# Layer 3's weight products in a four-layer graph kernel: ahead of layer 0, or in pieces inside its aggregation

## The chip, the cores and the metric

The kernel runs on one core of one Trainium2 chip. The metric is the device time of one execution in microseconds (us), less being better. TensorE (PE) does matmuls, VectorE (DVE) and ScalarE (ACT) work on vectors, GpSimd (POOL) on vectors and transfers, and SyncE (SP) sends most transfers (DMAs).

## The reference

Four graph layers work on x (2708 x 512, fp32) with one adjacency matrix adj (2708 x 2708, 0 or 1). Each normalizes x by rows, applies a relu, and adds its result to x. Cut to what matters here:

```python
# layer 0, h = relu(layernorm(x))
x = x + relu(((adj.T @ h) @ weight) * in_degree ** -0.5)
# layer 3, deg = rows' sums of adj
agg = adj @ h / deg
self_f = h @ W_self + b_self
nb_f = agg @ W_nb + b_nb
x = x + relu(concat(self_f, nb_f) @ W_comb + b_comb)
```

Nothing but linear steps lies between `W_self` or `W_nb` and `W_comb`. So the kernel makes the products `W_self @ W_comb[:512]` and `W_nb @ W_comb[512:]` once (each 512 x 512 x 512, fp32) and one row of bias, and layer 3 multiplies with these.

## The kernel before

`fast_layers` cuts the 2708 nodes into 22 chunks of 126 rows (NC = 22, R = 126; the last has 62). D = 512 columns make NF = 4 blocks of 128.

**Ahead of layer 0** (lines 321 to 375). A pool "pre" takes `W_self`, `W_comb`, `W_nb` and the biases. `turn_weight` transposes one weight: four blocks on TensorE into one PSUM bank (L341), and a copy by ACT to `wsT` (L342), four times. `fuse` makes 128 rows of one product in four fp32 matmuls (L347), and DVE copies them to `wf` (L354). When a product is whole, POOL's queue sends it to `fused` in DRAM (L356, 1 MB). DVE sums the rows of `W_comb`, weighted by the biases, into `part` (L367, L369), TensorE adds its partitions (L373), and the row goes to `bias3` (L375). Layer 3 reads `fused` and `bias3` some 800 us later.

**Layer 0** (lines 467 to 668) has six groups of column chunks, of 4, 4, 4, 4, 3 and 3 chunks; in the text they are groups 1 to 6 (g = 0 to 5 in the code). One unit is a group and a row chunk m: 6 x 22 = 132 units. `staged` calls every stage with a lag: at step s, a stage of lag k handles unit s - k. `load0` (lag 0) brings the adjacency tile `ai`, 126 rows by the group's columns, int32, from ten buffers. `count0` (lag 4) makes the matmul weight `ar` of it on ACT (L523), and on DVE a running count (L529), a degree (L537) and a packed pair of rows `two` (L541). `sign0` (lag 5) counts on ACT (L557). `multiply0` (lag 7) sends `two` to DRAM by POOL's queue (L574) and multiplies `ar` with the chunk's features into one PSUM accumulator per column chunk (L403, two matmuls each since a feature is held as a high and a low half). In the first group only, `dense` also runs: load x (lag 0), normalize (lag 1: L216, L218, L220, L221, L230), transpose on TensorE with a relu on ACT (lag 2: L239, L241), and multiply with the layer's weight `w0s` (lag 3: L186, four fp32 matmuls), then the two halves (L292 on ACT, L293 on DVE). At the end of a group the accumulators are scaled and added to x (L611 to L648); `fenced` puts the next group's `count0` and `sign0` behind these instructions on DVE and ACT.

**What orders the work.** The code gives a sequence and priorities. A scheduler simulates the program when it is built, and gives each engine and each queue a fixed order: what is ready goes, the earlier in the code the sooner. Work from far down can so come early. In the run each engine takes its order strictly, and a transfer waits in its queue until its buffer is free, with all behind it. The PSUM pool `ps` has eight banks, shared by accumulators, transposes and products.

**Layer 1's start** (lines 670 to 769) needs the degrees of all chunks: they go to DRAM and back (L685 to L692), and DVE waits for them at L695.

Of the kernel before, what the change touches and what calls it, by code (L numbers as in the profile page):

```python
# [20 lines left out]
P = 128  # L21
# [23 lines left out]
def fast_layers(  # L45
# [278 lines left out]
    with tc.tile_pool(name="pre", bufs=2) as pre:  # L324
        ws = [load_weight(pre, w_self, "ws")]
        wc = load_weight(pre, w_comb, "wc", k=2 * NF)
        ws.append(load_weight(pre, w_nb3, "ws"))
        bc = load_row(pre, b_comb, "bc")
        bcol = pre.tile([P, 2 * NF], F32, name="bcol")
        for i, b in enumerate((b_self, b_nb3)):  # L330
            nc.sync.dma_start(
                bcol[:, i * NF : (i + 1) * NF], b.rearrange("(k p) -> p k", p=P)
            )
        wsT = [pre.tile([P, NF, D], F32, name="wsT") for _ in range(2)]
        wf = [pre.tile([P, NF, D], F32, name="wf") for _ in range(2)]

        def turn_weight(i):
            for f in range(NF):
                pt = ps.tile([P, NF, P], F32, name="wsT_ps", tag="ps")
                for k in range(NF):  # L340
                    nc.tensor.transpose(pt[:, k, :], ws[i][:, f, k * P : (k + 1) * P], ident)  # L341
                nc.scalar.copy(wsT[i][:, :, f * P : (f + 1) * P], pt)  # L342

        def fuse(i, f):
            po = ps.tile([P, D], F32, name="fused_ps", tag="ps")
            for k in range(NF):
                nc.tensor.matmul(  # L347
                    po,
                    wsT[i][:, k, f * P : (f + 1) * P],
                    wc[:, i * NF + k, :],  # L350
                    start=(k == 0),
                    stop=(k == NF - 1),
                )
            nc.vector.tensor_copy(wf[i][:, f, :], po)  # L354
            if f == NF - 1:
                nc.gpsimd.dma_start(fused[i].rearrange("(k p) o -> p k o", p=P), wf[i])  # L356

        turn_weight(0)
        for f in range(NF):
            if f == NF // 2:  # L360
                turn_weight(1)
            fuse(0, f)
        for f in range(NF):
            fuse(1, f)

        part = pre.tile([P, D], F32, name="part", bufs=1)
        nc.vector.tensor_scalar(part, wc[:, 0, :], bcol[:, 0:1], None, op0=ALU.mult)  # L367
        for k in range(1, 2 * NF):
            nc.vector.scalar_tensor_tensor(  # L369
                part, wc[:, k, :], bcol[:, k : k + 1], part, op0=ALU.mult, op1=ALU.add  # L370
            )
        pb = ps.tile([P, D], F32, name="bias3_ps", tag="ps")
        nc.tensor.matmul(pb[:1], ones, part, start=True, stop=True)  # L373
        nc.vector.tensor_tensor(bc[:1], pb[:1], bc[:1], ALU.add)
        nc.gpsimd.dma_start(bias3, bc[:1])  # L375
# [76 lines left out]
    with ExitStack() as ring_ctx:  # L452
# [14 lines left out]
        w0s = load_weight(weights, w0, "w0s", tag="w")  # L467
# [10 lines left out]
        def product0(c, xc, hT, n):  # L478
            po = ps.tile([P, D], F32, name="h0_ps", tag="ps")
            any_product(c, po, hT, w0s, n)  # L480
            h0[c] = halves(ring, po, c)

        with tc.tile_pool(name="l0", bufs=2) as wk:
# [173 lines left out]
            def first_dense(lag, fn):  # L657
                return lag, lambda i: fn(i) if i < NC else None

            staged(  # L660
                len(units),
                (0, load0),
                *[first_dense(lag, fn) for lag, fn in dense(x_in, product0, rows_of=paired)],
                (4, fenced(count0)),
                (5, fenced(sign0)),
                (7, save0),
# [1365 lines left out]
```

## Time and profile before

| What | us |
|---|---|
| Median of 3 runs | 1805.42 |
| Lowest and highest run | 1805.1, 1805.82 |
| Span of the profiled execution, first to last instruction | 1804.1 |
| TensorE busy in it | 1767.0 |
| DVE, ACT, POOL busy | 1308.8, 815.3, 247.3 |
| First matmul; first transpose of layer 0 | 3.37; 38.78 |
| First adjacency tile sent | 47.64 |
| First accumulation matmul of layer 0 | 59.56 |
| Last accumulation matmul of layer 0 starts | 376.92 |

The page has no device time of its own for the profiled execution; its span is 1.3 us below the median. Each digit in the slices of the page is the busy share, in tenths, of a fortieth of the span (45.1 us). A line of a timeline has the start, the duration, the engine, the line of code, the operation, what it writes and reads, and how many instructions were merged; brackets hold the idle time of the engine before it, and what released it. Matmuls are pipelined, so the durations of single ones overlap, and a rate is read from a run of them.

### The profile page before, as it was taken

What the parts mean: (1) busy time and instruction counts of PE and PEld (TensorE: products, weight loads), DVE (VectorE), ACT (ScalarE), POOL (GpSimd) and SP (SyncE); (2) the same over time, 40 slices, a digit from 0 to 9 for tenths busy, and PEclk for the clock granted to TensorE, in tenths of its full rate; (3) what the DMA queues carried; (4) which work ended last, traced back from release to release, by engine and by line L of the source; (5) the groups of instructions that cost most, each with busy time, mean ns of one, the idle gap of its engine ahead of it and who ended that gap; (6) DMA issues with size and microseconds to landing.
All of it is one profiled execution on the core that took longest, in us unless ns stands there. A gap on an engine that the chain in (4) does not pass through costs nothing.

```text
span 1804.1 us, 30724 instructions
## 1 busy us (share of the span) xinstructions
PE 1767.0 (98%) x11880; PEld 1039.3 (58%) x11880; DVE 1308.8 (73%) x1842; ACT 815.3 (45%) x1554; POOL 247.3 (14%) x245
## 2 busy tenths in 40 slices
PE   9899999899999999999999999999999899999998
PEld 4456777654447887744444344344444445588776
DVE  4952998855546665788989999999999777633334
ACT  2643777731210000056887777767774566400000
POOL 0100332311110211157000000000000222100000
PEclk9999999999999999999999999999999999999999
DMA  7632666735552221243320220121122444313221
GB/s 249 191 103 80 205 207 188 216 72 123 122 123 62 62 69 53 66 154 107 102 62 13 57 60 24 47 62 43 28 63 56 137 138 134 116 33 105 70 69 45
DMA packets 165737, 176.62 MB, mean 98 GB/s; under 512 B 94890, under 2 KB 116100, under 8 KB 164700
## 3 DMA queue, kind: packets, MB, share of 16 engines
q1 hardware_dynamic: 143170, 131.47, 26.4%
q10 hardware_dynamic: 18668, 33.28, 5.4%
q0 software_dynamic: 3744, 9.82, 1.6%
q8 instruction: 95, 1.56, 0.4%
q14 instruction: 60, 0.49, 0.1%
HBM read 111.35 MB, written 55.15 MB: 92 GB/s over the span
## 4 chain that ended last, share of the span: by engine, by line
PE 80%; DVE 10%; issue 4%; DMA 4%; ACT 1%; POOL 0%; SPq 0%; DVEq 0%; ACTq 0%; POOLq 0%
PE acc L403 32%; PE av L1110 16%; PE nb_ps L186 7%; PE sums L1110 5%; DVE t L923 5%; PE self_ps L186 4%; PE line_ps L186 4%; PE wh_ps L186 3%; PE h_ps L186 3%; DVE cum L529 2%; PE hT_ps L239 2%; PE fused_ps L347 2%; DMA x<-x 1%; DMA ai<-in_adj 1%; DMA x<-in_x 1%
## 5 line engine op out<-in xcount | busy, mean ns | idle before, releaser
L923 DVE SCALAR_TENSOR_TENSOR t<-rb,ec,vT 126x2708 f32<-126x2708 f32 (+2 forms) x220 | 529.5, 2464 | 13.4 <-PE sums L1110 7.7
L403 PE MATMUL acc<-halves,kt 126*126 126x512 f32 x1848 | 435.7, 395 | 2.3 <-DVE kt L777 2.0
L1110 PE MATMUL av<-t,whs 126*32 126x451 f32 (+3 forms) x4576 | 433.5, 513 | 0.6 <-DVE ln_mv L218 0.6
L403 PEld LDWEIGHTS acc<-halves,kt 126*126 126x126 f32 x1848 | 342.6, 186 | 91.7 <-DVE kt L777 6.8
L1110 PEld LDWEIGHTS av<-t,whs 126*32 126x32 f32 (+1 forms) x4576 | 162.4, 110 | 200.7 <-issue 175.2
L403 PE MATMUL acc<-halves,ar 126*126 126x512 f32 x924 | 232.3, 404 | 3.4 <-ACT ar L523 2.0
L941 ACT ACTIVATE b<-t,eb 126x2708 bf16<-126x2708 f32 (+3 forms) x91 | 217.8, 2393 | 34.6 <-DVE t L923 32.9
L403 PEld LDWEIGHTS acc<-halves,ar 126*126 126x126 f32 x924 | 169.0, 186 | 53.8 <-issue 7.6
L220 ACT ACTIVATE ln_rs<-ln_mv,eps 126x1 f32<-126x1 f32 x88 | 25.6, 293 | 327.5 <-DVE ln_mv L218 323.3
L777 DVE SCALAR_TENSOR_TENSOR kt<-lastr,index,vT 126x504 fp32r<-126x504 int16 (+3 forms) x154 | 110.7, 731 | 78.6 <-PE acc L403 78.2
L1349 DVE CAST kt<-vT 126x504 fp32r<-126x504 uint8 (+3 forms) x154 | 56.1, 366 | 137.0 <-PE acc L403 137.0
L1077 POOL TENSOR_SCALAR z<-y 126x512 f32<-126x512 f32 x22 | 44.0, 2000 | 652.8 <-DVE y L1070 644.1
L1110 PE MATMUL sums<-t,whs 126*32 126x338 f32 (+4 forms) x1464 | 129.6, 447 | 2.7 <-ACT out L1151 2.7
L529 DVE TENSOR_TENSOR_SCAN cum<-ai,deg 126x504 int16<-126x504 int32 (+2 forms) x110 | 128.5, 1181 | 0.7 <-DMA ai<-in_adj 0.7
L911 ACT ACTIVATE whs<-wh,ef 126x64 f32<-126x64 f32 x220 | 76.6, 348 | 101.2 <-PE sums L1110 47.0
L557 ACT ACTIVATE cum<-cum,limit 126x504 int16<-126x504 int16 (+3 forms) x132 | 88.1, 668 | 58.9 <-DVE deg L537 57.9
L216 DVE BATCH_NORM_STATS2 ln_st<-x 126x6 f32<-126x512 f32 x88 | 60.4, 686 | 45.7 <-DMA x<-x 29.7
L1110 PEld LDWEIGHTS sums<-t,whs 126*32 126x32 f32 (+1 forms) x1464 | 52.6, 109 | 65.1 <-issue 35.9
L186 PE MATMUL h_ps<-w0s,hT 128*126 128x512 f32 x168 | 79.0, 614 | 5.5 <-ACT hT L241 4.2
L186 PE MATMUL nb_ps<-wfn,hT 128*126 128x512 f32 x168 | 75.7, 593 | 3.2 <-ACT hT L241 3.2
L186 PE MATMUL nb_ps<-wn,hT 128*126 128x512 f32 x168 | 76.6, 599 | 0.0
L523 ACT ACTIVATE ar<-ai 126x504 fp32r<-126x504 int32 (+2 forms) x132 | 74.9, 567 | 3.0 <-DMA ai<-in_adj 3.0
(202 smaller groups left out, 1885.6 us busy)
## 6 DMA issues: line engine op xcount, KB each, us to landing
x<-x SPq DMA_DIRECT2D x105, 252.0 KB
x<-x ACTq DMA_DIRECT2D x84, 252.0 KB
ai<-in_adj SPq DMA_DIRECT2D x84, 249.0 KB
x<-in_x SPq DMA_DIRECT2D x42, 252.0 KB
rb<-rT SPq DMA_DIRECT2D x7, 1332.8 KB
wh<-whd SPq DMA_DIRECT2D x70, 94.5 KB
packed<-two POOLq DMA_DIRECT2D x44, 124.5 KB, 4.4
whd<-wh SPq DMA_DIRECT2D x21, 252.0 KB
```

The source lines that it names most:

```text
L186: nc.tensor.matmul(po[:n], lhsT[:, f, :n], w[:, f, :], start=(f == 0), stop=(f == NF - 1))
L216: nc.vector.bn_stats(st[:n], xc[:n])
L403: nc.tensor.matmul(acc[:R], weight[:, k * R : (k + 1) * R], parts[:, i, :], start=(m == 0 and i == 0), stop=(m == NC - 1),)
L523: nc.scalar.activation(ar[:, :gw], ai[:, :gw], AF.Square, accum_out=squares[:R, m, g : g + 1])
L529: nc.vector.tensor_tensor_scan(cum[:n, :gw], ai[:n, :gw], ai[:n, :gw], 0.0 if g == 0 else deg[:n, m : m + 1], op0=ALU.add, op1=ALU.max,)
L557: nc.scalar.activation(cum[:n, :gw], cum[:n, :gw], AF.Sign, bias=limit[:n], scale=-1.0, accum_out=signs[:n, m, g : g + 1],)
L777: nc.vector.scalar_tensor_tensor(by_chunk(kt, cs), lastr[:, cs[0] * R : (cs[-1] + 1) * R].rearrange("p (c r) -> p c r", r=R), index[:R, m ...
L911: ins = nc.scalar.activation(t[:q, :O], wh.pop((u, m))[:q], AF.Copy, scale=by)
L923: ins = nc.vector.scalar_tensor_tensor(t[:q, : hi - lo], row[h][:q, lo:hi], ec[:q, m, h : h + 1], vT[g][:q, k, lo:hi], op0=ALU.max, op1=AL ...
L941: nc.scalar.activation(b[:q, : hi - lo], weight[s][:q, : hi - lo], AF.Sigmoid, bias=eb[:q, m, h : h + 1], scale=STEEP,)
L1110: nc.tensor.matmul(p[j * S : (j + 1) * S, : b - a], lhsT, rhs[:, part * size + a : part * size + b], start=(s % NC == 0), stop=(s % NC == ...
L1349: nc.vector.tensor_copy(by_chunk(kt, cs), pattern(m, cs))
```

## The change

The pool "pre" and its block go. A class `Fusion` holds the same work in pieces: `load`, `turn` (four transposes and an ACT copy), `multiply` (one fp32 matmul; the fourth of a row block also copies the block by ACT, not DVE, and sends its 256 KB on POOL's queue), `add` (one step of the bias row on DVE), `close`. Its buffers are single, except for `wf` with two, and lie beside layer 0's in a pool of their own. A table assigns pieces to units, and a last stage of lag 7 runs them after `multiply0` of that unit: product i = 0 in groups 2 and 3 (4 turns and 8 multiplies, then 8 multiplies), product i = 1 in groups 4 and 5 in the same way, from the third step of a group to its eighteenth; the adds in the last four units of groups 1 and 3; the close in group 6. The weights of a product are asked for ten units ahead of its first group. `w0s` is loaded in the first step, after the first x chunk and before the first adjacency tile; x comes ahead of adj in every step of the first group.

```diff
@@ -321,58 +321,65 @@
 
     bias3 = dram.tile([1, D], F32, name="bias3")
     fused = [dram.tile([D, D], F32, name=f"fused{i}") for i in range(2)]
-    with tc.tile_pool(name="pre", bufs=2) as pre:
-        ws = [load_weight(pre, w_self, "ws")]
-        wc = load_weight(pre, w_comb, "wc", k=2 * NF)
-        ws.append(load_weight(pre, w_nb3, "ws"))
-        bc = load_row(pre, b_comb, "bc")
-        bcol = pre.tile([P, 2 * NF], F32, name="bcol")
-        for i, b in enumerate((b_self, b_nb3)):
-            nc.sync.dma_start(
-                bcol[:, i * NF : (i + 1) * NF], b.rearrange("(k p) -> p k", p=P)
+
+    class Fusion:
+        def __init__(self, pool):
+            self.pool = pool
+            self.ws, self.wc, self.wsT, self.po = {}, {}, {}, {}
+
+        def load(self, i):
+            self.ws[i] = load_weight(self.pool, (w_self, w_nb3)[i], "ws")
+            self.wc[i] = load_weight(self.pool, w_comb[i * D : (i + 1) * D, :], "wc")
+            if i == 0:
+                self.bcol = self.pool.tile([P, 2 * NF], F32, name="bcol")
+                for j, bias in enumerate((b_self, b_nb3)):
+                    nc.sync.dma_start(
+                        self.bcol[:, j * NF : (j + 1) * NF], bias.rearrange("(k p) -> p k", p=P)
+                    )
+                self.bc = self.pool.tile([1, D], F32, name="bc")
+                nc.sync.dma_start(self.bc, b_comb.rearrange("(o d) -> o d", o=1))
+
+        def turn(self, i, f):
+            if f == 0:
+                self.wsT[i] = self.pool.tile([P, NF, D], F32, name="wsT")
+            pt = ps.tile([P, NF, P], F32, name="wsT_ps", tag="ps")
+            for k in range(NF):
+                nc.tensor.transpose(pt[:, k, :], self.ws[i][:, f, k * P : (k + 1) * P], ident)
+            nc.scalar.copy(self.wsT[i][:, :, f * P : (f + 1) * P], pt)
+
+        def multiply(self, i, f, k):
+            if k == 0:
+                self.po[i, f] = ps.tile([P, D], F32, name="fused_ps", tag="ps")
+            po = self.po[i, f]
+            nc.tensor.matmul(
+                po,
+                self.wsT[i][:, k, f * P : (f + 1) * P],
+                self.wc[i][:, k, :],
+                start=(k == 0),
+                stop=(k == NF - 1),
             )
-        wsT = [pre.tile([P, NF, D], F32, name="wsT") for _ in range(2)]
-        wf = [pre.tile([P, NF, D], F32, name="wf") for _ in range(2)]
-
-        def turn_weight(i):
-            for f in range(NF):
-                pt = ps.tile([P, NF, P], F32, name="wsT_ps", tag="ps")
-                for k in range(NF):
-                    nc.tensor.transpose(pt[:, k, :], ws[i][:, f, k * P : (k + 1) * P], ident)
-                nc.scalar.copy(wsT[i][:, :, f * P : (f + 1) * P], pt)
-
-        def fuse(i, f):
-            po = ps.tile([P, D], F32, name="fused_ps", tag="ps")
-            for k in range(NF):
-                nc.tensor.matmul(
-                    po,
-                    wsT[i][:, k, f * P : (f + 1) * P],
-                    wc[:, i * NF + k, :],
-                    start=(k == 0),
-                    stop=(k == NF - 1),
-                )
-            nc.vector.tensor_copy(wf[i][:, f, :], po)
-            if f == NF - 1:
-                nc.gpsimd.dma_start(fused[i].rearrange("(k p) o -> p k o", p=P), wf[i])
-
-        turn_weight(0)
-        for f in range(NF):
-            if f == NF // 2:
-                turn_weight(1)
-            fuse(0, f)
-        for f in range(NF):
-            fuse(1, f)
-
-        part = pre.tile([P, D], F32, name="part", bufs=1)
-        nc.vector.tensor_scalar(part, wc[:, 0, :], bcol[:, 0:1], None, op0=ALU.mult)
-        for k in range(1, 2 * NF):
+            if k == NF - 1:
+                wf = self.pool.tile([P, D], F32, name="wf", bufs=2)
+                nc.scalar.copy(wf, self.po.pop((i, f)))
+                nc.gpsimd.dma_start(fused[i][f * P : (f + 1) * P, :], wf)
+
+        def add(self, i, k):
+            col = self.bcol[:, i * NF + k : i * NF + k + 1]
+            if (i, k) == (0, 0):
+                self.part = self.pool.tile([P, D], F32, name="part")
+                nc.vector.tensor_scalar(self.part, self.wc[i][:, k, :], col, None, op0=ALU.mult)
+                return
             nc.vector.scalar_tensor_tensor(
-                part, wc[:, k, :], bcol[:, k : k + 1], part, op0=ALU.mult, op1=ALU.add
+                self.part, self.wc[i][:, k, :], col, self.part, op0=ALU.mult, op1=ALU.add
             )
-        pb = ps.tile([P, D], F32, name="bias3_ps", tag="ps")
-        nc.tensor.matmul(pb[:1], ones, part, start=True, stop=True)
-        nc.vector.tensor_tensor(bc[:1], pb[:1], bc[:1], ALU.add)
-        nc.gpsimd.dma_start(bias3, bc[:1])
+
+        def close(self):
+            pb = ps.tile([P, D], F32, name="bias3_ps", tag="ps")
+            nc.tensor.matmul(pb[:1], ones, self.part, start=True, stop=True)
+            nc.vector.tensor_tensor(self.bc, pb[:1], self.bc, ALU.add)
+            nc.gpsimd.dma_start(bias3, self.bc)
 
 
 
@@ -464,7 +471,7 @@
             ],
         )
 
-        w0s = load_weight(weights, w0, "w0s", tag="w")
+        w0_of = []
         h0 = {}
         l1_weights = []
         sums1 = {}
@@ -477,10 +484,10 @@
 
         def product0(c, xc, hT, n):
             po = ps.tile([P, D], F32, name="h0_ps", tag="ps")
-            any_product(c, po, hT, w0s, n)
+            any_product(c, po, hT, w0_of[0], n)
             h0[c] = halves(ring, po, c)
 
-        with tc.tile_pool(name="l0", bufs=2) as wk:
+        with tc.tile_pool(name="l0", bufs=2) as wk, ExitStack() as ctx_l0:
             units = [(g, m) for g in range(len(groups)) for m in range(NC)]
             tiles, uppers, acc, sums, xs = {}, {}, {}, {}, {}
 
@@ -657,15 +664,46 @@
             def first_dense(lag, fn):
                 return lag, lambda i: fn(i) if i < NC else None
 
+            def load_w0(i):
+                if i == 0:
+                    w0_of.append(load_weight(weights, w0, "w0s", tag="w"))
+
+            fusion = Fusion(ctx_l0.enter_context(tc.tile_pool(name="fusion", bufs=1)))
+            pieces_at = {}
+
+            def at(i, fn, *args):
+                pieces_at.setdefault(i, []).append((fn, args))
+
+            for i in range(2):
+                first_unit = (1 + 2 * i) * NC
+                at(first_unit - 10, fusion.load, i)
+                steps = [(fusion.turn, i, f) for f in range(NF)]
+                steps += [(fusion.multiply, i, f, k) for f in range(NF) for k in range(NF)]
+                for g, own in enumerate((steps[:12], steps[12:])):
+                    for n, step in enumerate(own):
+                        at(first_unit + g * NC + 2 + n * (NC - 5) // len(own), *step)
+                for k in range(NF):
+                    at(first_unit - 4 + k, fusion.add, i, k)
+            at(5 * NC + 2, fusion.close)
+
+            def fuse0(i):
+                for fn, args in pieces_at.pop(i, ()):
+                    fn(*args)
+
+            first = [first_dense(lag, fn) for lag, fn in dense(x_in, product0, rows_of=paired)]
             staged(
                 len(units),
+                first[0],
+                (0, load_w0),
                 (0, load0),
-                *[first_dense(lag, fn) for lag, fn in dense(x_in, product0, rows_of=paired)],
+                *first[1:],
                 (4, fenced(count0)),
                 (5, fenced(sign0)),
                 (7, save0),
                 (7, multiply0),
+                (7, fuse0),
             )
+            assert not pieces_at
 
         vpool = ctx.enter_context(tc.tile_pool(name="vpool", bufs=1))
         vT.extend(
```

## Prediction

> **What bounds the kernel now.** I read the page's slices first, then TensorE's timeline of the head and of layer 0, then busy time by stage, then the chain of work that ended last.
>
> ```profile
> PE   9899999899999999999999999999999899999998
> DVE  4952998855546665788989999999999777633334
> PEclk9999999999999999999999999999999999999999
> ```
>
> TensorE (PE) is busy in every slice, 1767.0 of 1804.1 us. Moving its work can therefore gain only what is now idle or slow on it, some 37 us over the whole kernel, unless its busy time is not real work. A slice is 45 us: the 8 in the second one is layer 0's first group. Now the head, on the chain that ended last:
>
> ```profile
> 1.65 3.97 DMA ws<-in_L_gnn_W_self
> 5.67 1.97 PE wsT_ps L341 x8
> 7.64 7.91 PE fused_ps L347 x16
> 15.55 1.75 PE wsT_ps L341 x16
> 17.30 20.60 PE fused_ps L347 x48
> 37.90 0.96 PE bias_ps L373 x2
> ```
>
> The columns are start, duration, work. From 5.67 to 38.9 us the chain is the weight products without a break. The warm rates are in it: 20.60 / 48 = 0.429 us for one fused record (each fp32 matmul leaves two records, 64 for 32 matmuls), 1.75 / 16 = 0.109 us for a transpose. Then layer 0's first group on TensorE's timeline, only the lines that begin with an idle stretch (its length and releaser in brackets):
>
> ```profile
> 40.11 3.70 PE L186 MATMUL h_ps<-w0s,hT 128*126 128x512 f32 x8 [0.25 <-ACT hT L241]
> 52.56 3.70 PE L186 MATMUL h_ps<-w0s,hT 128*126 128x512 f32 x8 [0.58 <-ACT hT L241]
> 69.41 3.67 PE L186 MATMUL h_ps<-w0s,hT 128*126 128x512 f32 x8 [1.28 <-DVE deg L537]
> 78.78 6.63 PE L186 MATMUL h_ps<-w0s,hT 128*126 128x512 f32 x8 [3.41 <-ACT hT L241]
> 105.61 0.65 PE L239 MATMUL hT_ps<-ident,hn 126*128 126x126 f32 x4 [0.45 <-DVE halves L293]
> ```
>
> The stall of 3.41 us is followed by eight matmuls in 6.63 us where the chain has 3.44 for the same eight: the array ran at half rate. Last, busy time in groups 2 to 4 (168 to 299 us) and group 5 (304.6 to 341.9 us), in columns PE, PE weight loads, DVE, ACT, POOL, granted clock, DMA share and GB/s; then group 5's three stalls:
>
> ```profile
> 168.00:299.00 131.00, 131.00 (x794) 100.82 (x792) 112.87 (x172) 94.10 (x271) 39.59 (x48) 1.00 0.67 206
> 304.60:341.90 37.30, 34.31 (x199) 25.17 (x198) 31.64 (x66) 26.91 (x93) 13.06 (x19) 1.00 0.62 179
> ```
>
> ```profile
> 313.01 3.16 PE L403 MATMUL acc<-halves,ar 126*126 126x512 f32 x12 [0.66 <-ACT ar L523]
> 327.11 3.22 PE L403 MATMUL acc<-halves,ar 126*126 126x512 f32 x12 [1.35 <-ACT ar L523]
> 337.80 0.23 PE L592 MATMUL sums_ps<-ar,oneb 62*32 62x126 bf16 x3 [0.98 <-ACT ar L523]
> ```
>
> TensorE never stops in groups 2 to 4. Group 5 has three chunks instead of four, so less TensorE work a step, and there it waits for the adjacency tiles that ACT and DVE prepare.
>
> **What the Trainium skill says.** "TensorE: Matmul & The Clock Gate", Part 1: the array starts at half clock, reaches full clock after some 3.4 us of sustained work, and falls back after an idle window of that length. The trace agrees: 6.63 against 3.44 us after the 3.41 us stall, and transposes of 1.97 / 8 = 0.246 us at the start against 0.109 later. "DMA: Bandwidth & Descriptors", Issuing engines are not separate DMA queues: all transfers share the same 16 engines and interleave. Here an x chunk issued at 70.45 us took 6.12 us, on the chain, behind a burst of adjacency tiles. "Perfetto Trace Analysis", Identifying the Most-Contended Engine: matmul busy time is no measure of how near TensorE is to its limit. So I compare rates: 7.63 / 32 = 0.238 us per accumulation matmul in groups 2 to 4, and 38.62 / 166 = 0.233 us in layer 1's aggregation (from 621.65 us), where DVE has no scans to do. The two lie 2.4% apart: groups 2 to 4 are bound by TensorE.
>
> **The change, part by part.**
>
> 1. *The products leave the head.* Warm, they are 32 x 0.109 = 3.5 us of transposes, 64 x 0.429 = 27.5 us of matmuls, 0.96 us of bias: 31.9 us of TensorE work. The head took 38.78 us (start of layer 0's first transposes), so it lost 38.78 - 31.9 = 6.8 us to the first DMA (3.37 us) and to cold or waiting matmuls. This work is moved, not removed.
>
> 2. *Layer 0 starts cold and alone.* First loss: the head start. The first 256 KB chunk lands near 3.4 us, as the first piece of ws does now. Stats 0.70, aggregate 0.19, square root 0.3, reciprocal 0.17, scale 0.54, with gaps of 0.3: hn at 5.6 us. Transposes (0.4), the relu on ACT (0.58) and the last piece of w0, the fifth transfer in the queue, put the first product near 7.3 us, a further loss of 1.2. The half clock lasts into this product: 2.3 us, between 1.5 and 3.5. Then stalls of the ramp: now 0.25 + 0.58 + 1.28 + 3.41 + 0.45 = 6.0 us, and 3.2 us for the cold matmuls behind the long one, 9.2 in all. Their cause goes away in part: the twelve adjacency loads wait until 47.64 us now, since their buffers lie where the head's pool was, and then come in one burst; afterwards they are issued between the x chunks from the start. A dense step needs some 500 KB and takes 3.9 to 5.7 us of TensorE, while the transfers ran at 274 and 346 GB/s in the first 20 us (500 KB in 1.5 to 1.8 us). I take 2 us of stalls, from 0 to 8, since ws and wc (2 MB), and layer 1's weights, which the scheduler sends at 17.59 us already now, share these 16 engines. After: 5.6 + 1.2 + 2.3 + 2 = 11.1 us lost, against 6.8 + 9.2 = 16.0. Gain 4.9 us.
>
> 3. *The pieces in groups 2 to 4.* Groups 2 and 4 get 4 turns (0.44 us each) and 8 multiplies (0.86 us each, two records), 8.6 us; group 3 gets 6.9 us. TensorE is full there: all of it lengthens the path, and is the same work that left the head. Nothing cancels.
>
> 4. *The eight multiplies in group 5*, 6.9 us, fall on steps 2 to 16, between the waits of 0.66, 1.35 and 0.98 us. Each gives ACT and DVE 0.86 us more every other step: the three stalls go, 3.0 us gained (at least 1).
>
> 5. *The copies and the row.* The eight wf copies move from DVE (0.68 us) to ACT (0.59 us); with the eight wsT copies ACT gets 9.4 us in groups 2 to 5. ACT is 94.1 of 131 us busy in 2 to 4, and steps get longer. An ACT copy waits for its piece, and the ar of later steps is queued behind it, for which TensorE waits. Unpriced in this trace: between 0 (the lead covers it) and 3 us, I take 1. Nothing can be gained by a wait. DVE's eight adds (0.73 us) fall at the ends of groups 1 and 3, where DVE has room (12.0 of 20 us busy at 100 to 120; 112.9 of 131 later): 0. Without that cover, at most 5.8 us.
>
> 6. *Queues.* SP gets the loads of ws and wc in two sets in place of one; the second set waits for the first one's release, which could hold adjacency loads behind it, but ten buffers are some 20 us of lead: 0 (3 if not). POOL gets eight DMAs of 256 KB for two of 1 MB, 0.8 to 1.0 us each to issue as now (0.99, 0.78), among the packed writes; behind them DVE's two waits for one of three buffers. POOL is 39.6 of 131 us busy: 0.
>
> 7. *The close* in group 6: 0.68 us on DVE, which sets the end of that group (its last degree starts the degd transfer at 370.51 us); TensorE's 0.96 us fall in its stalls. Cost 0.5, from 0 to 0.7.
>
> Sum: -4.9 - 3.0 + 1.0 + 0.5 = -6.4 us. The profiled span is 1804.1 us, the median 1805.42, so 1.3 us lie around the span or between executions: 1797.7 + 1.3 = 1799.0 us.
>
> **Rivals.** *A blocked ramp (slower).* DVE and ACT work in order. Now, DVE's stats wait for an x chunk, ACT's sign behind them, the hT relu behind that, and TensorE for 1.28 + 3.41 us plus 3.2 cold: 7.9 us for one event. It was seen once with a head start of 38 us; without one, a late x has nothing in front of it. One event in place of my 2 us gives 1804.9 (no change); two give 1812.8. Slower from 1809: 12 us of stalls, one event and a half. For it: the ramp also carries 3 MB of other weights. Against: the burst that made x late is gone. 0.20 for one, 0.17 for two.
> *Free pieces.* If groups 2 to 4 were paced by DVE, their 24.1 us would vanish: 1775. Against it the rates above; 0.04.
> *The pieces don't stay there.* The scheduler moves ready work ahead: rdeg's memset of layer 1 runs at 1.84 us. Pieces pulled into the ramp fill its 2 us of stalls but leave group 5's 3.0: about 1800. 0.09.
>
> **How the numbers follow.** Forecast 0.50, from 1793.7 (no stalls or waits, short half clock, a start 1 us earlier) to 1810 (stalls 8, half clock 3.5, waits 3, group 5 giving 1). About 0.2%, 3.6 us, is what a measurement can tell: below 1801.8 faster, above 1809.0 slower. Faster: 0.45 of the forecast, 0.04 free, 0.06 pulled ahead: 0.55. Same: 0.05 + 0.17 + 0.03 = 0.25. Slower: 0.17 + 0.03 = 0.20. The range 1793 to 1810 leaves out the free case, most of two events, and a little below.
>
> **What would show it.** First h_ps near 7.3 us; the end of the last h_ps, now 166.5 us, 31.9 + 4.9 = 36.8 us earlier, near 130; groups 2 to 4 about 24 us longer in sum, without idle; no stalls in group 5. It is wrong if TensorE stalls for over 12 us before 130 us, if pieces run before 60 us, or if groups 2 to 4 grow by clearly more or less than 24 us.

## The result, and the profile after

The changed kernel takes 1804.93 us (median of 12 runs, 1799.7 to 1807.3); the kernel before took 1804.94 us beside it (12 runs). The ratio is 0.9999, 95% interval 0.9991 to 1.0006: no change. The profiled execution spans 1803.6 us and took 1805.35.

The slices of the page, changed kernel:

```profile
PE   7999999999999999999999999999999899999998
DVE  8726787855446655788989999999999777633334
```

The first two digits of PE tell the story that follows: the first slice fell from 9 to 7, the second rose from 8 to 9. TensorE is now idle for 12.6 of the first 45 us instead of 3.8, and for 4.2 of the second instead of 5.3. Next TensorE's timeline of the changed kernel, the head and all later lines of group 1 that begin with an idle stretch, with the first product and the one behind it for its rate:

```profile
6.88 1.07 PE L239 MATMUL hT_ps<-ident,hn 126*128 126x126 f32 x4 [6.88 <-DVE hn L230]
13.62 1.10 PE L239 MATMUL hT_ps<-ident,hn 126*128 126x126 f32 x4 [5.67 <-DVE hn L230]
14.51 6.20 PE L186 MATMUL h_ps<-w0s,hT 128*126 128x512 f32 x8
...
20.98 3.60 PE L186 MATMUL h_ps<-w0s,hT 128*126 128x512 f32 x8
...
51.07 3.67 PE L186 MATMUL h_ps<-w0s,hT 128*126 128x512 f32 x8 [1.17 <-DVE halves L293]
...
58.58 0.65 PE L239 MATMUL hT_ps<-ident,hn 126*128 126x126 f32 x4 [1.42 <-DVE deg L544]
...
65.11 0.65 PE L239 MATMUL hT_ps<-ident,hn 126*128 126x126 f32 x4 [0.58 <-DVE halves L293]
66.82 5.39 PE L186 MATMUL h_ps<-w0s,hT 128*126 128x512 f32 x8 [1.06 <-ACT hT L241]
```

The first product starts at 14.51 us, not 7.3. TensorE's fixed order is transposes of chunk 0, transposes of chunk 1, first product, so the product stands behind chunk 1's normalize. Why that is late, DVE's and ACT's timelines of the same stretch show, lines picked from each:

```profile
3.36 0.69 DVE L216 BATCH_NORM_STATS2 ln_st<-x 126x6 f32<-126x512 f32 x1 [3.36 <-DMA x<-in_x]
...
9.32 1.21 DVE L536 TENSOR_TENSOR_SCAN cum<-ai 126x504 int16<-126x504 int32 x1 [2.60 <-DMA ai<-in_adj]
...
10.71 0.68 DVE L216 BATCH_NORM_STATS2 ln_st<-x 126x6 f32<-126x512 f32 x1
...
13.03 0.53 DVE L230 TENSOR_SCALAR hn<-x,ln_mv,ln_rs 126x512 f32<-126x512 f32 x1
```

```profile
4.36 1.28 ACT L220 ACT_TABLE_LOAD   x1 [4.36 <-DVE ln_mv L218]
...
9.38 0.62 ACT L530 ACTIVATE ar<-ai 126x504 fp32r<-126x504 int32 x1 [3.43 <-DMA ai<-in_adj]
...
11.96 0.61 ACT L530 ACTIVATE ar<-ai 126x504 fp32r<-126x504 int32 x1
...
12.69 0.59 ACT L241 ACTIVATE hT<-hT_ps 128x504 f32<-128x504 f32 x1
```

DVE waits for adjacency tile 0 and scans it (L536) ahead of the statistics of x chunk 1 (L216). ACT makes two `ar` tiles, which nobody uses before 35.6 us, ahead of the relu of chunk 0 (L241), which TensorE needs now: its transposes were done at 7.95 us, the relu ran at 12.69. Both engines take counts of tiles, which TensorE multiplies only seven steps after their load, ahead of dense work. The 1.28 us of a table load also lie ahead of chunk 0's normalize; I had not counted them.

Last, busy time by group in the changed kernel, with the ends of groups 1 to 6 as edges (columns as in the prediction):

```profile
150.00:202.00 52.00, 52.00 (x296) 38.23 (x295) 39.03 (x60) 34.94 (x99) 14.34 (x18) 1.00 0.67 206
202.00:251.00 49.00, 49.00 (x275) 35.41 (x274) 41.75 (x62) 32.74 (x93) 14.37 (x18) 1.00 0.69 218
251.00:303.00 52.00, 52.00 (x297) 38.16 (x296) 37.88 (x59) 34.24 (x98) 14.36 (x18) 1.00 0.56 169
303.00:342.60 39.60, 39.60 (x212) 27.84 (x211) 31.89 (x65) 28.03 (x95) 14.23 (x21) 1.00 0.61 186
342.60:376.80 34.20, 34.20 (x203) 25.72 (x202) 28.00 (x80) 23.33 (x85) 12.39 (x24) 1.00 0.46 136
```

TensorE has no idle time from group 2 to the end of layer 0. Each group ends with the turn of its column sums (L607 before, L614 after). Their starts give the ledger:

| Stretch, us | before | after | difference |
|---|---|---|---|
| start to end of group 1 | 175.72 | 149.67 | -26.05 |
| groups 2, 3, 4 | 42.93, 42.96, 42.96 | 51.61, 49.86, 51.62 | +24.24 |
| group 5 | 37.00 | 39.89 | +2.89 |
| group 6 | 36.06 | 34.24 | -1.82 |
| end of group 6 to end of span | 1426.5 | 1426.7 | +0.2 |

The pieces came back to within 1% of the 24.1 us forecast for groups 2 to 4. What failed is the first row: -36.8 was forecast.

### The profile page after: what moved, and what is told of

It reads as the page before. It is cut to its first block, busy times and chain, and to the rows that moved or that the text cites. A ratio compares the mean times of both kernels' runs of the same rounds, so it can differ in the third digit from the quotient of the medians.

```text
span 1803.6 us, 30726 instructions
## 1 busy us (share of the span) xinstructions
PE 1765.1 (98%) x11880; PEld 1037.9 (58%) x11880; DVE 1302.4 (72%) x1834; ACT 819.4 (45%) x1561; POOL 250.6 (14%) x251
## 4 chain that ended last, share of the span: by engine, by line
PE 86%; DVE 7%; DMA 2%; issue 2%; ACT 1%; SPq 0%; POOL 0%; DVEq 0%; ACTq 0%; POOLq 0%
PE acc L410 34%; PE av L1148 19%; PE nb_ps L186 8%; PE sums L1148 6%; PE wh_ps L186 4%; PE self_ps L186 4%; PE line_ps L186 4%; DVE t L961 3%; PE h_ps L186 3%; PE hT_ps L239 2%; PE fused_ps L356 2%; DVE cum L536 1%; DMA ai<-in_adj 1%; PE sums_ps L599 1%; PE av_ps L1101 0%
## 5 line engine op out<-in xcount | busy, mean ns | idle before, releaser
L410 PE MATMUL acc<-halves,ar 126*126 126x512 f32 x924 | 243.5, 413 | 0.0
L220 ACT ACTIVATE ln_rs<-ln_mv,eps 126x1 f32<-126x1 f32 x88 | 25.8, 295 | 303.1 <-DMA x<-x 197.9
L536 DVE TENSOR_TENSOR_SCAN cum<-ai,deg 126x504 int16<-126x504 int32 (+2 forms) x110 | 128.6, 1181 | 0.6 <-DMA ai<-in_adj 0.6
L216 DVE BATCH_NORM_STATS2 ln_st<-x 126x6 f32<-126x512 f32 x88 | 60.3, 685 | 39.5 <-DMA x<-x 26.3
```

The lines of the kernel that those rows point to most:

```text
L216: nc.vector.bn_stats(st[:n], xc[:n])
L410: nc.tensor.matmul(acc[:R], weight[:, k * R : (k + 1) * R], parts[:, i, :], start=(m == 0 and i == 0), stop=(m == NC - 1),)
L536: nc.vector.tensor_tensor_scan(cum[:n, :gw], ai[:n, :gw], ai[:n, :gw], 0.0 if g == 0 else deg[:n, m : m + 1], op0=ALU.add, op1=ALU.max,)
```

## The experiments

Theory A: the start loses its gain because chunk 1's normalize and chunk 0's relu stand behind early adjacency work on DVE and ACT. Rivals: the table load; the transfers (x, w0 and the adjacency tiles share the engines, and other weights come at 33 to 53 us); pieces that are free; products that belong in the head. Each ratio is to the kernel before, measured beside it, with its 95% interval; "faster" and "slower" say that the interval leaves out 1. Unless it says otherwise, an edit is made on the changed kernel.

**Adjacency loads three steps later.**

```diff
-                (0, load0),
+                (3, load0),
```

> Theory A (the ramp decides): in the changed kernel the first product of layer 0 waits in TensorE's order behind the second transposes (13.62 us), which wait for the second x chunk's stats; in DVE's order these stand behind the count of adjacency tile 0, which lands at 9.3 us, and on ACT the relu of the first chunk stands behind two adjacency squares. With the adjacency loads three steps later, TensorE's order stays as it is; the first product starts at 9 to 10 us instead of 14.5, the last h_ps of group 1 ends 4 to 5 us earlier (near 136) and the whole is 4 us faster, 1800.9 us. Theory B (the ramp is not on the path to the end; the degrees' path at the end of layer 0 or a later wait is): the last h_ps moves as in A, the time stays within 1 us of the changed kernel's 1804.9. Theory C (half clock and DVE's load set the ramp, not the order): the first product is earlier by under 2 us, or later stalls grow by as much: 1804.

Measured: 1801.89 us, ratio 0.9981 [0.9974, 0.9989], faster. TensorE's order is the same, instruction by instruction. The transfers come in another order, and with them DVE and ACT: both now take chunk 1's statistics and square root ahead of the first count. TensorE's timeline, picked lines:

```profile
11.54 1.10 PE L239 MATMUL hT_ps<-ident,hn 126*128 126x126 f32 x4 [3.85 <-DVE hn L230]
12.43 4.77 PE L186 MATMUL h_ps<-w0s,hT 128*126 128x512 f32 x8
...
48.23 5.39 PE L186 MATMUL h_ps<-w0s,hT 128*126 128x512 f32 x8 [1.83 <-ACT hT L241]
...
63.78 3.70 PE L186 MATMUL h_ps<-w0s,hT 128*126 128x512 f32 x8 [1.04 <-ACT hT L241]
```

The first product comes 2.1 us sooner, at 12.43 us and not at 9 to 10; stalls of 1.83 and 1.04 us remain, and they wait for ACT's relu. This is part of the cause, and the transfers' share is not yet told from that of the order on DVE and ACT.

**The table load ahead of x.**

```diff
-    nc.gpsimd.memset(eps, EPS)
+    nc.gpsimd.memset(eps, EPS); nc.scalar.activation(const.tile([P, 1], F32, name="warm"), eps, AF.Sqrt)
```

> The activation table is loaded by a dummy square root before x arrives; in the changed kernel it stands at 4.36 to 5.66 us on the way to the first normalized chunk. Theory A: the first transposes start at 5.6 us instead of 6.88, but TensorE's second transposes still wait for adjacency tile 0 in DVE's order, so the first product stays at 14.5 us and the time within 0.5 us of 1804.9. If the table load itself is what the forecast missed: the first product and the whole are 1.3 us earlier, 1803.6.

Measured: 1805.39 us, 1.0008 [0.9997, 1.0019]. The first transposes start at 5.28 us instead of 6.88, the second ones still at 13.67: the table load is hidden behind the wait for chunk 1.

**Both, and w0 one step later.**

```diff
-                (0, load_w0),
-                (0, load0),
+                (1, load_w0),
+                (3, load0),
```

> Adjacency loads three steps later, the activation table early, and the layer's weight one step later, behind the second x chunk. Theory A: second x chunk lands near 4 to 5 us, the weight near 8, the first product starts at 8 to 8.5 us; the last h_ps of group 1 ends 6 us earlier than in the changed kernel and the whole is 6 us faster, 1799. Theory B: 1804.9. If the weight's later arrival costs what x gains: as with adjacency later alone, 1801.

Measured: 1803.09 us, 0.9996 [0.9985, 1.0007]: a miss. Layer 0 ends 6.0 us sooner than in the changed kernel (370.87 against 376.89), as expected, but the profiled execution's rest took 1429.7 us instead of 1426.7. It has a spell of half-rate matmuls at the start of layer 3, which the last section takes up; nothing in the edit explains it. The run says that the head can be shortened, and nothing safe on the whole. The first product starts at 11.02 us and not at 8 to 8.5, and its lines show why (TensorE's, then ACT's):

```profile
11.02 5.09 PE L186 MATMUL h_ps<-w0s,hT 128*126 128x512 f32 x8 [2.98 <-ACT hT L241]
...
10.06 0.29 ACT L220 ACTIVATE ln_rs<-ln_mv,eps 126x1 f32<-126x1 f32 x1 [4.19 <-DVE ln_mv L218]
10.38 0.59 ACT L241 ACTIVATE hT<-hT_ps 128x504 f32<-128x504 f32 x1
```

Chunks 0 and 1 are both transposed by 8.04 us, and no count stands in front. But ACT's order has the square root of chunk 2 (L220) ahead of the relu of chunk 0 (L241), and it waits for statistics of an x chunk that DVE takes up at 9.00 us. So dense work of a later chunk blocks too, not only counts.

**No products.**

```diff
-            for i in range(2):
+            for i, w in enumerate((w_self, w_nb3)):
+                at((1 + 2 * i) * NC, nc.gpsimd.dma_start, fused[i], w)
+            at(5 * NC + 2, nc.gpsimd.dma_start, bias3, b_comb.rearrange("(o d) -> o d", o=1))
+            for i in range(0):
...
-            at(5 * NC + 2, fusion.close)
```

> Leaves out the weight products: fused and bias3 are filled with copies of W_self, W_nb and b_comb, so layer 3's result is another. Theory A (groups 2 to 5 are bound by TensorE, the pieces cost their own time less the stalls of groups 5 and 6 that they fill): 31.9 us of TensorE work goes, 3 us of stalls in group 5 and up to 2 in group 6 come back, ramp as in the changed kernel: 1804.9 - 27 = 1778 us. Rival (pieces are hidden behind DVE or ACT): 1803 to 1805. If the ramp's late stalls (50 to 67 us) come from the products' weights and adds, group 1 also ends up to 4 us earlier: 1774.

Measured: 1780.45 us, 0.9860 [0.9844, 0.9876]. Groups 2 to 4 take 42.9 us each again, and the stalls of group 5 (0.65, 0.90, 0.48, 0.98 us) and of group 6 (0.85, 1.82) are back. So the pieces cost what TensorE needs for them, less the stalls that they fill; that they are free is refuted. The idle time before chunk 1's transposes is there too, 9.98 us where the changed kernel has 5.67, so the pieces are not what holds the head.

**ws, wc and layer 1's weights behind the last x chunk** (with the adjacency loads later).

```diff
+                    with tc.issue_after(loads[NC - 1]):
+                        l1_weights.extend(
...
+            def load_behind(i):
+                with tc.issue_after(loads[NC - 1]):
+                    fusion.load(i)
...
-                at(first_unit - 10, fusion.load, i)
+                at(first_unit - (10 if i else 6), load_behind, i)
```

> As e1 (adjacency three steps later), and the loads of the first product's weights and of layer 1's weights are queued on SP behind the last x chunk of group 1, so that 3 MB and the four adds of the bias row leave the time from 33 to 67 us. Theory A1 (late stalls of the ramp come from these transfers and adds): the stalls between 45 and 67 us, 3.2 us in e1 with 2 us at half clock behind them, fall below 1.5 us, the last h_ps ends 3 us earlier than in e1, the time is 1799 us. Theory A2 (they come from DVE, which is full of counts that run ahead of need): they stay within 1 us of e1's, 1801.9 us.

Measured: 1805.27 us, 0.9992 [0.9982, 1.0002]. The ramp's stalls stay (1.26, 0.70, 0.95, 1.53 us) with 3 MB of transfers out of their way and the early adds gone with them. Transfers of other weights and DVE's adds are refuted as their cause. TensorE also waits 2.14 us early in layer 1, while DVE waits for the degrees' way to DRAM and back (13.09 us); the kernel with one product ahead, below, has 1.95 us at the same place with layer 1's weights where they were, so the weights are not the reason.

**The first product ahead of chunk 1's transposes** (with the adjacency loads later).

```diff
-                *first[1:],
+                first[1],
+                first[3],
+                first[2],
```

> As e1, and in each step the product of a chunk stands ahead of the transposes of the next one in the program. If TensorE's order (second transposes ahead of the first product) is what is left of the late start in e1: the first product starts at 8.5 to 9.5 us instead of 12.4, the time falls by 2 to 3 us to 1799.5. If ACT's order holds it (relu of the first chunk behind the square roots of the second and third): first product within 1 us of e1's, 1802. If the relu between transposes and product is then exposed in every dense step (0.6 us each): the ramp ends later than in e1 by 2 us or more, 1804.

Measured: 1812.95 us, 1.0035 [1.0023, 1.0047], slower. Its first product, and a later one:

```profile
12.03 6.40 PE L186 MATMUL h_ps<-w0s,hT 128*126 128x512 f32 x8 [3.66 <-ACT hT L241]
...
31.27 3.70 PE L186 MATMUL h_ps<-w0s,hT 128*126 128x512 f32 x8 [2.03 <-ACT hT L241]
```

The product moved up by 0.4 us only: now it waits for ACT's relu, at 11.39 us in this run and right behind the square root of a later chunk at 11.07. In later steps too the relu is no longer covered by the next chunk's transposes: five of them wait 1.0 to 2.3 us for it before 60 us. TensorE's own order alone was not the culprit. What is late is late on ACT and DVE.

**All pieces, or one product, back in front of layer 0**, from the changed kernel's buffers.

```diff
+            early = [(fn, args) for i in sorted(pieces_at) for fn, args in pieces_at[i] if True]
+            for i in pieces_at:
+                pieces_at[i] = [p for p in pieces_at[i] if p not in early]
+            for fn, args in early:
+                fn(*args)
```

In the second kernel the condition is `args and args[0] == 0`: product 0 ahead, product 1 in groups 4 and 5.

> All pieces are issued ahead of layer 0, as in the kernel before, but from the buffers of the changed kernel, which lie beside layer 0's; so adjacency tiles can land during the products. If the ramp of the kernel before lost its 9.2 us to the adjacency tiles that waited for the head's buffers: the products take 37 to 40 us (3 us for single buffers), layer 0's first group then runs with under 3 us of stalls, the end of group 1 comes 4 to 6 us earlier than before; groups 5 and 6 have their 5.2 us of stalls again: 1800 us. If the stalls came from DVE's order and load: 1805 or more.

> Product 0 is issued ahead of layer 0 and fills TensorE while x and adjacency tiles land; product 1 stays in groups 4 and 5. Theory A (what counts is TensorE's lost time in the ramp plus the stalls of groups 5 and 6): first matmul at 3.4 us, head loss 6 to 7 us, stalls after it 3 us or less, so some 10 us lost against 17 in e1 and 22 in the changed kernel; groups 5 and 6 without stalls: 1795 to 1797 us, the fastest. Rival (x comes late behind 3 MB of weights and TensorE idles between product 0 and the first dense step): 1802 or more.

Measured: all ahead 1817.02 us, 1.0057 [1.0040, 1.0073]; one ahead 1803.28 us, 0.9980 [0.9971, 0.9989]. All ahead, TensorE waits 8.89 us for the second `wc`, whose single buffer is loaded late, and 4.55 us for ACT's relu. One ahead, product 0 runs from 3.59 to 21.5 us, and then TensorE idles 7.41 us for chunk 0's relu (29.15 us), which stands in ACT's order behind the counts of seven adjacency tiles and the last copy of a `wf`. I took the counts for the cause, and tried the order itself.

**The order in group 1.** The last normalize on DVE and the last relu on ACT are remembered, and the next tile's counts are put behind them, by the means that already orders them behind a group's end. No other edit is made; the scheduler then plans anew.

```diff
-        nc.vector.tensor_scalar(
+        marks["dve"] = nc.vector.tensor_scalar(
             hn[:n], xc[:n], mv[:n, 0:1], rs[:n], op0=ALU.subtract, op1=ALU.mult
-        )
+        ).ins
...
-        nc.scalar.activation(hT[:, :, :n], pt[:, :, :n], AF.Relu)
+        marks["act"] = nc.scalar.activation(hT[:, :, :n], pt[:, :, :n], AF.Relu).ins
...
+                (4, lambda i: fences.update(marks) if i < NC else None),
                 (4, fenced(count0)),
```

Three kernels got it: the one with product 0 ahead (with the adjacency loads later as well), the one with the adjacency loads later, and the changed kernel as it is.

> Product 0 ahead of layer 0 as in e8, adjacency loads three steps later as in e1, and in group 1 the squares and counts of a unit are ordered on ACT and DVE behind the relu and the normalizing of chunks two and three further, so that they can't stand before dense work. In e8 TensorE waited 7.41 us for the first relu, which stood behind squares and signs on ACT, and ran the first product at half clock (6.40 us). If ACT's order is the cause: the first product starts at 23 to 24 us instead of 29.8, at full clock, the last h_ps starts 9 to 11 us earlier than in e8 (148.75), near 139, and the time is 0.993 of the kernel before. If x's late arrival is the cause: the wait stays over 5 us and the time at 0.998.

> e1 with the same order of squares and counts behind dense work in group 1. Theory A2 (the ramp's stalls at 45 to 67 us come from counts and squares that DVE and ACT take ahead of need, in an order fixed before the run): the three stalls (3.2 us) and the half clock behind them (2 us) go, the last h_ps starts at 129 instead of 133.8 us, 0.9955 of the kernel before. Otherwise (transfers late, or DVE simply full): stalls of over 2 us stay, 0.998.

> The changed kernel with that order alone, adjacency loads where they were. If order alone is the cause of both the late first product (14.5 us) and the later stalls: first product at 10 to 11 us (the second x chunk now lands behind the weight and adjacency tile 0, not behind its count), last h_ps near 130 instead of 138.6, 0.9955 of the kernel before. If the transfers' order matters beside it: the first product starts at over 12 us, 0.998.

Measured: one ahead and order 1798.89 us, 0.9963 [0.9949, 0.9977]; loads later and order 1795.86 us, 0.9950 [0.9938, 0.9963]; the order alone 1795.99 us, 0.9950 [0.9937, 0.9963]. The order alone gives 9 us, and later adjacency loads, worth 3 us without it, give nothing on top.

With one product ahead the expectation was missed: the first product starts at 28.95 us instead of 29.79, not at 23 to 24, and TensorE still waits 4.64 us for the relu. ACT's lines:

```profile
27.82 0.59 ACT L366 COPY wf<-fused_ps 128x512 f32<-128x512 f32 x1 [3.67 <-DMA fused<-wf]
28.30 1.08 ACT L242 ACTIVATE hT<-hT_ps 128x504 f32<-128x504 f32 x2
```

The relu stands behind a copy to `wf` that waits until one of its two buffers has gone to DRAM. So the counts were not most of the 7.41 us there. TensorE's timeline with the order alone; it has no other line with an idle stretch until layer 1:

```profile
6.89 1.07 PE L240 MATMUL hT_ps<-ident,hn 126*128 126x126 f32 x4 [6.89 <-DVE hn L230]
11.78 1.10 PE L240 MATMUL hT_ps<-ident,hn 126*128 126x126 f32 x4 [3.82 <-DVE hn L230]
12.68 5.81 PE L186 MATMUL h_ps<-w0s,hT 128*126 128x512 f32 x8
```

All four later stalls are gone, and with them the second half-rate spell: 4.2 and 1.8 us of the 9.1 us by which group 1 ends sooner. The head gives much less. The first product starts at 12.68 us instead of 14.51, over the 12 us at which the expectation had the transfers matter too. Chunk 1's statistics still wait until 9.60 us, for x itself, and TensorE waits 3.82 us for that chunk. With the adjacency loads later and the order the wait is 3.81 us, so adjacency tiles in between are not what holds it; with w0 queued behind chunk 1 (the third experiment) the same statistics ran at 4.64 us. And chunk 0's relu (10.97 us) still stands behind chunk 1's square root (10.66).

**The control: the same order in the kernel before.** If the order were what the change lacked, the kernel before should not profit from it.

> The kernel before, with the same order of ACT and DVE in group 1 as in the run with the order alone. Theory A (the order's gain has nothing to do with the change; it removes the stalls of any ramp): the stalls of 0.58, 1.28, 3.41 and 0.45 us and the 3.2 us of half rate behind the long one go, some 8 us: time about 1797.5, ratio about 0.9955, and the change with the order is then worth 1 to 2 us of its own. Theory B (the long stall of the kernel before comes from an x chunk that lands late behind the burst of adjacency loads, and no order of ACT and DVE makes it land sooner; only the change, which gives the adjacency loads their buffers from the start, removed it): only the 0.58 and 0.45 us go, the 1.28 and 3.41 us and the half rate stay: ratio 0.999 to 1.001, and the change with the order is worth some 8 us. In between, 0.997 to 0.999, part of each.

Measured: 1797.77 us, 0.9947 [0.9933, 0.9960]. It profits just as much. Its TensorE timeline, all idle stretches of groups 1, 5 and 6 but the 3.56 us at the start, and below it the one line of SP's queue with the burst of adjacency loads:

```profile
38.70 3.70 PE L186 MATMUL h_ps<-w0s,hT 128*126 128x512 f32 x8 [0.25 <-ACT hT L242]
...
50.95 3.70 PE L186 MATMUL h_ps<-w0s,hT 128*126 128x512 f32 x8 [0.39 <-ACT hT L242]
...
303.02 3.17 PE L404 MATMUL acc<-halves,ar 126*126 126x512 f32 x12 [0.67 <-ACT ar L524]
...
316.93 3.25 PE L404 MATMUL acc<-halves,ar 126*126 126x512 f32 x12 [1.18 <-ACT ar L524]
...
327.63 0.23 PE L593 MATMUL sums_ps<-ar,oneb 62*32 62x126 bf16 x3 [0.96 <-ACT ar L524]
...
343.09 0.22 PE L593 MATMUL sums_ps<-ar,oneb 126*32 126x126 bf16 x1 [0.84 <-DVE ar L528]
...
347.33 3.50 PE L404 MATMUL acc<-halves,ar 126*126 126x512 f32 x14 [1.49 <-DVE deg L538]
```

```profile
46.39 7.19 SPq L101 DMA_DIRECT2D ai<-in_adj  x12
```

The stalls of 1.28 and 3.41 us and the half rate are gone although the burst of twelve loads is still there. So the burst did not cause them; my prediction had said that it did. What did, the kernel before shows in these lines of DVE, SP's queue and ACT:

```profile
69.89 0.53 DVE L230 TENSOR_SCALAR hn<-x,ln_mv,ln_rs 126x512 f32<-126x512 f32 x1
70.45 0.32 SPq L101 DMA_DIRECT2D x<-in_x  x1
...
77.44 0.71 ACT L557 ACTIVATE cum<-cum,limit 126x504 int16<-126x504 int16 x1 [2.40 <-DVE deg L537]
78.15 0.57 ACT L241 ACTIVATE hT<-hT_ps 128x504 f32<-128x504 f32 x1
```

An x chunk goes out 0.03 us after a normalize on DVE has ended (70.42 us here), so DVE's order, with counts in between, sets when x is sent. And the relu for which TensorE waits 3.41 us stands behind a count on ACT, which waits for DVE's degree, which stands behind the statistics of that late x (76.60 us). Between 40 and 90 us SP's longest wait for a normalize was 11.3 us; with the order it is 4.7 us. From 62 to 97 us x then goes out every 4.7 to 5.5 us, where the kernel before took 6.7 to 8.5 us. The late x was a result of the order.

Side by side, ends in us:

| | group 1 ends | layer 0 ends | groups 2 to 6 |
|---|---|---|---|
| before | 175.72 | 377.63 | 201.91 |
| after | 149.67 | 376.89 | 227.22 |
| before, with the order | 165.50 | 367.58 | 202.08 |
| after, with the order | 140.58 | 367.97 | 227.39 |

In both pairs the change takes 25 or 26 us from group 1 and gives 25.3 back in groups 2 to 6. Of the 10.2 us that the order takes from group 1 in the kernel before, 1.4 lie in the head, where layer 0's first transposes start at 37.37 instead of 38.78 us: the first 16 records of the products took 7.10 us for 8.12, so full rate came sooner in that execution, which the order does not explain. With the order the two ratios to the kernel before, 0.9950 and 0.9947, lie inside each other's intervals: as without it, the change is worth nothing that these runs can tell, within some 0.2%. The two were not run side by side.

## Why the prediction was right or wrong

The range held the time, and the likeliest case did not come: 1799.0 and "faster" were forecast, 1804.93 and no change came. Step by step:

- **Step 1, the products** (31.9 us): right; without them the kernel is 25 us faster and not 32. In its profiled execution groups 2 to 5 give back 27.0 us, while group 6, whose stalls return, and group 1 take 5.2 more.
- **Step 2, the ramp: this failed.** "After: 5.6 + 1.2 + 2.3 + 2 = 11.1 us lost, against 6.8 + 9.2 = 16.0. Gain 4.9 us." By the end of group 1 it lost 16.0 + 31.9 - 26.05 = 21.8 us. The terms that the timeline shows: the head 14.51 less 0.9 of warm transposes, 13.6 us for 6.8; the half clock 6.20 - 3.60 = 2.6 us for 2.3; stalls 1.17 + 1.42 + 0.58 + 1.06 = 4.2 us and 5.39 - 3.60 = 1.8 us of half rate behind them, 6.0 us for 2. In sum 22.2. Two reasons fail in it. I followed chunk 0 alone (5.6 + 1.2), not what DVE, ACT and TensorE have queued in front of its product: chunk 1's square root and transposes, and counts. Of the 6.8 us by which the head missed, moving the counts back gives 1.8. The other 5.0 stay: chunk 0's transposes start 1.3 us later than the 5.6 (6.89, with the table load), and the product then waits for chunk 1. And I took transfer time alone for the pace of the ramp, and read the kernel before's long stall as a late x behind a burst; with the order put right, the burst stays and the stall goes, and in the changed kernel all 6.0 us of stalls and half rate. With the order, group 1 ends at 140.58 us, and the forecast makes 175.72 - 36.8 = 138.9. That these lie within 1.7 us is in part luck: the head still lost 5.0 us more than forecast, and the ramp had none of the 2 us of stalls.
- **Step 3, groups 2 to 4**: 24.1 forecast, 24.24 measured, no idle time.
- **Step 4, group 5**: its three stalls went, as forecast; 2.89 us for 6.9 - 3.0 = 3.9.
- **Steps 5 and 7**: nothing of the 1.0 us for ACT's waits nor of the 0.5 us for the close was seen. Group 6 lost its stalls of 0.84 and 1.37 us too, which I had not counted on. Four of DVE's adds ran at 62 to 66 us, in the ramp, not at the end of group 1; with them and their loads moved out, the stalls stayed, so "0" holds, with another reason.
- **Step 6, queues**: 0, no sign of another value in the groups' lengths.

The sum by the table: -26.05 + 25.31 = -0.74 us, where my terms make -36.8 + 31.0 - 3.0 + 1.0 + 0.5 = -7.3 (0.9 below my -6.4, which gave nothing for the bias matmul that vanishes in group 6's stalls). Step 2 was 10.7 us too good, and steps 4, 5 and 7 with group 6's stalls some 4.2 us too bad. That the range held owes something to this: two errors of opposite sign.

**The rivals.** "A blocked ramp" with one event, at 1804.9 us and 0.20, is where it landed; that it fits to 0.1 us is luck, as the sums above show. Its mechanism, DVE and ACT working in order, is shown for the later stalls: they and their half rate, 6.0 us, go with the order. What blocks there is counts taken ahead, and a late x follows from them. More than half of the miss lies in the head, which the rival did not have; there the counts make 1.8 us. The rest stands behind chunk 1's work in the orders of ACT and TensorE; no run put both of these right, so that share is read from the timelines and not shown by a run. "Free pieces" was refuted by leaving the products out. Pieces pulled ahead were not seen.

**Why the change is worth nothing even with the order**: the head before was not all waste. While TensorE made products, the first x chunks, w0 and their normalizing went on beside it. With the order on both sides, the products' head loses 37.37 - 31.9 = 5.5 us (1.4 less than without the order, see above) and 0.6 of stalls; the other waits 12.68 - 0.9 = 11.8 us for its first product and 2.2 us at half clock. By the ends of group 1 the difference is 31.9 - 24.9 = 7.0 us (the visible terms make 7.9). Against it stand the stalls of groups 5 and 6 that the pieces fill, 0.67 + 1.18 + 0.96 + 0.84 + 1.49 = 5.1 us, and some 1.5 us more (31.9 - 5.1 - 25.3), nearly all in groups 5 and 6, that I can't place.

**Open.** Whether DVE's or ACT's order matters more was not separated. No run has both the order and the head put right: w0 behind chunk 1, and chunk 0's relu and product ahead of later chunks' work. The rest of the kernel after layer 0 took 1426.2 us with the order alone and 1429.3 us for the kernel before with it. The record of the granted clock accounts for that: apart from the last 6 us of both, it shows half clock for 3.4 us there in the first (from 993.3 us) and for 3.4 and 6.8 us in the second (from 385.4 and 1392.4 us). If half clock costs half its time, the difference is 3.4 us by this estimate, against 3.1 measured. So one profiled execution can't tell such differences from an edit, and the verdicts rest on the ratios.

## What to carry to other kernels

Work at the head that looks like an unhidden prologue may be the cover for the first loads and normalizations: count what its removal uncovers before counting what it frees. For a start, write down the fixed order of each engine and ask of every instruction ahead of the critical one when its result is needed; in a fixed order, work done early for a later step can be a wait for the step that is due. And run the remedy on the old kernel too: here an order found while looking for the change's lost gain was worth 9 to 10 us, and owed nothing to the change.

## What the hardware showed that was not expected

TensorE's half rate came after shorter stalls than the 3.41 us of the kernel before: eight matmuls took 5.39 us after 1.83 us idle (adjacency loads later), and 5.39 us after 1.42, 0.58 and 1.06 us within ten (changed kernel), while 2.03 us in the kernel with the product first was followed by 3.70 us. The Trainium skill, "TensorE: Matmul & The Clock Gate", Part 1, has the clock fall after an idle window of some 3.4 us; these stalls are shorter, so the length of the last stall alone did not decide here.

Nor did the edit. All 14 profiled executions have the same stall of 1.82 or 1.83 us at the start of layer 3. In ten of them the next eight records of `nb_ps` took 3.70 us, in four 4.98 to 6.19 us. First the order alone, then the kernel before with the order:

```profile
1389.98 0.62 PE L240 MATMUL hT_ps<-ident,hn 126*128 126x126 f32 x4 [1.83 <-DVE hn L230]
...
1392.95 3.70 PE L186 MATMUL nb_ps<-wfn,hT 128*126 128x512 f32 x8
...
1390.43 0.62 PE L240 MATMUL hT_ps<-ident,hn 126*128 126x126 f32 x4 [1.83 <-DVE hn L230]
...
1394.36 6.08 PE L186 MATMUL nb_ps<-wfn,hT 128*126 128x512 f32 x8
```

The mean granted clock is 1.00 from 1389.9 to 1397.0 us in the first and 0.50 from 1392.4 to 1399.1 us in the second. This is the spell of the third experiment as well. What starts it in one execution and not in another stays open.

The load of ACT's table took 1.28 us, as "ScalarE: Activation LUTs", What ACT_TABLE_LOAD costs, has it (1283 ns). The page adds some 1380 ns of drain for every switch to a different set; none was seen between load and square root, neither at the first load (4.36 us, square root at 5.66) nor at a second one in the kernel with one product ahead (13.17 us, square root at 14.46). ACT had been idle before both.
